# Attention with ALiBi beside a mixture of experts: the order of matmuls in a step, a ring of eight PSUM banks, and values added up in SBUF

## The chip, the core and the metric

The kernel runs on one core of a Trainium2 chip. The metric is device time in microseconds (us); lower is better. Three runs of the kernel before took 1695.01, 1697.31 and 1699.47 us, so the median is 1697.31.

## What is computed

Input `x` has 4 sequences of 1024 tokens with 512 features, all in float32. It is normalized (layer norm without weights), and two branches work on the normalized rows; their outputs are added to the input:

```
xn = layernorm(x)
q, k, v = xn @ Wq.T + bq, ...                    # 16 heads of 32
scores = q @ k.T / sqrt(32); causal mask; scores += -slope[h] * |i - j|
attention = softmax(scores) @ v, heads joined, @ Wo.T + bo
probs = softmax(xn @ gate_w.T); the best 2 of 8 experts, weights scaled to sum 1
expert(t) = (silu(g) * u) @ w2.T,  g, u = split(xn @ w1.T)     # 352 wide
result = x + attention + sum over 2 experts of weight * expert
```

## The kernel before

**Units and groups.** After the norm and the routing, attention runs in 16 units (b, c): a sequence and a chunk of 4 heads (4 x 32 = 128 partitions). A unit has 12 steps, g = 0 to 11. In each step the kernel works on three things of the attention:

- `largest` (L833) for the *next* unit: scores with queries on the partitions, tiles `m`, four matmuls, one per head (L843). A block of 128 queries needs one group of up to 512 keys, or two. DVE adds the distances, takes the least value per query and writes the sum `z` to SBUF (L860). When a block is complete, ACT computes the exponentials of `z` with their sums (`sums`, L880); only the sums are wanted. They go into three bf16 terms each, for shift and inverse (`finish_largest`, `split`, L909), which TensorE turns (`turn_largest`, tile `pt`, L929) into `mT`.
- `scores` (L938): scores with keys on the partitions, tiles `s`, four matmuls (L947), then two kinds of bf16 matmuls that add the shift from `mT` (L958 on the diagonal, L966 with `ones_b`). ACT takes the exponentials (`pr`, L978); on the diagonal POOL clears what is masked (L986).
- `values` (L1015) of the group of the step before: four matmuls that multiply `pr` with the values and add up in one PSUM bank `o` over all groups of a block of 512 queries (L1029). With the last group, `spread_inverse` (L998) spreads the inverses of the sums over the heads' partitions (tile `pi`, four small matmuls, L1003, and a DVE copy `inv`, L1012), and DVE writes `oT = o * inv` (L1039).

The widths differ by step. `s` has 512, 384, 256 and 128 columns in steps 0 to 3, 512 in steps 4 to 8, then 384, 256 and 128. `m` has 128, 256, 384 and 512 in steps 0 to 3, then 512 and 128, 512 and 256, 512 and 384, 512 and 512.

**Shapes on TensorE.** The matmuls of `s` and `m` contract over 32 rows and fill 128 columns (32x128 in the profile); the four heads use the four row strips side by side. `o` contracts over 128 rows and fills 32 columns a head (128x32). All else is 128x128. Every f32 product is two passes in the profile.

**Other work ("fills").** Everything else that TensorE has to do is cut into pieces with estimated lengths: for each of 71 blocks of 128 routed rows `gate` (2.9 us, with the turning of the previous block's activations, `pact`), `up` (2.4) and `second_layer` (3.3: turning of the next rows, `pxs`, and the product `ye` of the block before); the projections of queries, keys and values of later units (`todo`, 3.6 each); and at the end the output projections (3.6) and the joining of expert results on DVE (1.5). A planner, `fill` (L1114), spreads them evenly over gaps, two per step: it keeps a running target (`rate` times the number of gaps) and takes the next piece when the target is reached. The projections of 3.6 are generators that stop halfway (`yield`), so that one half goes into a gap and the other into the next.

**The order of a step** is written out by hand (L1218 to L1230), and each engine follows the program's order: `scores`, `values` of the group before, a gap, the sums on ACT, `largest`, the terms that are due (`run_later`), a gap.

**PSUM.** It has eight banks. Seven are a ring (pool `ps_s`, tag `s`): every tile takes the next one and waits until the tile that had it seven allocations before has been read. The eighth (`ps_o`) holds the routing table first and then `o`.

Of the kernel before, what the change touches and what calls it, by code (L numbers as in the profile page):

```python
# [28 lines left out]
def kernel(  # L29
# [83 lines left out]
    with ExitStack() as actx:  # L113
# [3 lines left out]
        ps_s = actx.enter_context(tc.tile_pool(name="ps_s", bufs=7, space=PSUM))  # L117
        ps_o = actx.enter_context(tc.tile_pool(name="ps_o", bufs=1, space=PSUM))
# [4 lines left out]
        def set_attention():  # L123
# [60 lines left out]
            pick_inv = wp.tile([P, D], BF16, tag="pick_inv", name="pick_inv")  # L184
            for h in range(HC):
                nc.gpsimd.memset(pick_inv[h * D : (h + 1) * D, :], 1.0)
                nc.gpsimd.memset(pick_inv[h * D : h * D + INV, :], 0.0)
# [23 lines left out]
        def project_bias():  # L211


            ps = ps_s.tile([P, E], F32, tag="s", name="pbv")
# [92 lines left out]
        def norm_turn(g):  # L307
# [7 lines left out]
            for n in range(LG):  # L315
                t = g * LG + n
                ptr = ps_s.tile([P, NC, P], F32, tag="s", name=f"ptr{t}")
# [9 lines left out]
        def norm_gate(g):  # L327
            xT = xTs.pop(g)
            plg = ps_s.tile([P, LG * P], F32, tag="s", name=f"plg{g}")
# [15 lines left out]
        def norm_top(g):  # L345
            lgT = lgTs.pop(g)
            plt = ps_s.tile([P, LG, NE], F32, tag="s", name=f"plt{g}")
# [48 lines left out]
        psum = ps_o.tile([P, QB], F32, tag="o", name="routing")  # L396
# [169 lines left out]
        def qk_pieces(b, c):  # L566
# [6 lines left out]
            def piece(which, s):  # L573
                ps = ps_s.tile([P, QB], F32, tag="s", name=f"p{which}_{b}_{c}_{s}")
                for i in range(NC):
# [7 lines left out]
                    if i == NC // 2 - 1:  # L583
                        yield
# [21 lines left out]
        def v_pieces(b):  # L606
            def piece(t):
                ps = ps_s.tile([P, E], F32, tag="s", name=f"pv_{b}_{t}")
                for i in range(NC):
# [7 lines left out]
                    if i == NC // 2 - 1:  # L617
                        yield
# [14 lines left out]
        def expert_pieces():  # L633
# [37 lines left out]
            def turn(k):  # L671
# [4 lines left out]
                ps = ps_s.tile([P, NC, P], F32, tag="s", name=f"pxs_{k}")  # L676
# [5 lines left out]
            def half_up(k, gu):  # L682

                ps = ps_s.tile([P, FI], F32, tag="s", name=f"p{('gate', 'up')[gu]}_{k}")
# [28 lines left out]
            def turn_act(k):  # L713
                if k < 0:
                    return
                ps = ps_s.tile([P, NF, P], F32, tag="s", name=f"pact_{k}")
# [10 lines left out]
            def down(k):  # L727
                if k < 0:
                    return
                y = ps_s.tile([P, E], F32, tag="s", name=f"ye_{k}")  # L730
# [36 lines left out]
        def final_pieces(b):  # L767
# [24 lines left out]
            def project(t, xr, lhsTs):  # L792
                y = ps_s.tile([P, E], F32, tag="s", name=f"y{t}")
                for c in range(NC):
                    nc.tensor.matmul(  # L795
                        y, lhsT=lhsTs[c], rhs=wo_sb[:, c, :], start=(c == 0), stop=(c == NC - 1)
                    )
                    if c == NC // 2 - 1:
                        yield
# [3 lines left out]
            def piece(i):  # L803
# [6 lines left out]
                if o is not None:  # L810
                    return project(t, xr, [o[:, c, :] for c in range(NC)])

            def rest(i):
                cols = slice((i % QT) * P, (i % QT + 1) * P)
                return project(
# [17 lines left out]
        def largest(b, c, g):  # L833
# [6 lines left out]
            for h in range(HC):  # L840
                r = slice(h * D, (h + 1) * D)
                ps = ps_s.tile([P, QB], F32, tag="s", name=f"m_{b}_{c}_{g}_{h}")
# [35 lines left out]
            def sums():  # L878
                for h in range(HC):
                    nc.scalar.activation(  # L880
                        z[h][:, :L],
                        z[h][:, :L],
                        AF.Exp,
                        bias=top[:, h : h + 1],
                        scale=-slopes[c * HC + h],
                        accum_out=total[:, i % QT, h : h + 1],
                    )

            late_sums.append(sums)
# [6 lines left out]
        def run_sums():  # L896
            while late_sums:
# [26 lines left out]
        def turn_largest(b, c, s):  # L924

            t3 = terms[s % 2]
            pt = ps_s.tile([P, QT, P], BF16, tag="s", name=f"pt_{b}_{c}_{s}")
# [10 lines left out]
        def scores(b, c, g):  # L938
# [5 lines left out]
            for h in range(HC):  # L944
                r = slice(h * D, (h + 1) * D)
                ps = ps_s.tile([P, QB], F32, tag="s", name=f"s_{b}_{c}_{g}_{h}")
# [50 lines left out]

        def spread_inverse(b, c, s):  # L998

            ps = ps_s.tile([P, QB], F32, tag="s", name=f"pi_{b}_{c}_{s}")  # L1000
            for h in range(HC):
                r = slice(h * D, h * D + INV + 3)
                nc.tensor.matmul(  # L1003
                    ps[h * D : (h + 1) * D, :],
# [274 lines left out]
```

## Time and profile before

The profiled execution took 1696.5 us; its span (first to last instruction) is 1694.8 us.

| | |
|---|---|
| median of three runs | 1697.31 us |
| profiled execution, its span | 1696.5, 1694.8 us |
| granted clock of TensorE, mean | 0.996 |
| DVE, ACT, POOL busy in unit 5 (92.7 us) | 48.0, 52.5, 14.0 us |
| DVE, ACT, POOL busy in unit 14 (84.5 us) | 59.4, 46.9, 45.9 us |
| idle of TensorE in unit 14 | 4.3 us, nearly all in one wait for the tile `ot` |

In the profile PE is TensorE's matmuls and PEld its weight loads, DVE is VectorE, ACT ScalarE, POOL GpSimd. L947 is line 947 of the kernel. A timeline row gives the start and the length in us, then engine, line, operation, output and inputs, shape (rows*columns of the array, then partitions x columns of the moving operand) and the number of instructions merged. Matmuls overlap in the pipeline, so the length of a row reaches into the next one; the distance from start to start is what a block of matmuls takes. "Busy" counts those lengths, and waits shorter than a drain don't show in it. In the table of groups, the figures behind the bar are the total busy time, the mean length in ns and the idle time of the engine before the group, with what ended it.

### The profile page before, as it was taken

The page shows a single profiled execution, that of the slowest core. Times are in us where ns is not written, and L with a number is a line of the kernel's source. Part 1 is how long each engine was busy: PE and PEld are TensorE (multiplying, and loading weights), DVE is VectorE, ACT ScalarE, POOL GpSimd, SP SyncE. Part 2 cuts the span into 40 slices and gives each one's busy share as a digit, 9 for nine tenths or more (in the row PEclk, how much of TensorE's full clock was granted, in tenths as well). Part 3 has the DMA queues.
Part 4 walks back from the last instruction along what each step waited for, and adds up shares of the span by engine and source line. Part 5 has one row for each costly group of instructions (what it writes and reads, how often), then busy time and mean ns, then how long its engine had stood idle before and what let it go on. Part 6 is the DMA issues. An engine that isn't in the chain of part 4 may idle for free.

```text
span 1694.8 us, 29487 instructions
## 1 busy us (share of the span) xinstructions
PE 1671.3 (99%) x9572; PEld 735.4 (43%) x9572; DVE 914.1 (54%) x2944; ACT 886.7 (52%) x2074; POOL 339.0 (20%) x762
## 2 busy tenths in 40 slices
PE   7999999999999999999999999999999999989999
PEld 4555444444444444444444444444444444433333
DVE  7757555545554545546454545555454545548752
ACT  4353555565464555565455555555555556455531
POOL 5611102021111201021111202011111202035561
PEclk9999999999999999999999999999999999999999
DMA  9747645465343424465443434474434424448881
GB/s 315 312 138 259 213 140 181 157 207 192 129 146 111 126 92 143 154 222 178 135 139 110 130 102 144 140 234 167 147 127 122 135 82 134 135 141 257 245 279 63
DMA packets 146491, 278.99 MB, mean 165 GB/s; under 512 B 16448, under 2 KB 45120, under 8 KB 144800
## 3 DMA queue, kind: packets, MB, share of 16 engines
q1 hardware_dynamic: 132128, 234.60, 42.5%
q0 software_dynamic: 10800, 35.40, 6.9%
q10 hardware_dynamic: 3408, 7.10, 1.1%
q8 instruction: 76, 1.25, 0.3%
q14 instruction: 79, 0.65, 0.2%
HBM read 229.07 MB, written 47.97 MB: 163 GB/s over the span
## 4 chain that ended last, share of the span: by engine, by line
PE 96%; DVE 1%; DMA 1%; issue 1%; POOL 0%; ACT 0%; ACTq 0%; SPq 0%; DVEq 0%
PE ye L733 11%; PE pup L686 11%; PE pgate L686 10%; PE m L843 10%; PE s L947 10%; PE o L1029 9%; PE pk L576 7%; PE pq L576 7%; PE pv L610 7%; PE y L795 6%; PE pxs L679 2%; PE s L966 2%; PE pact L719 2%; PE pt L929 1%; PE pi L1003 1%
## 5 line engine op out<-in xcount | busy, mean ns | idle before, releaser
L978 ACT ACTIVATE pr<-s,kbias 128x512 f32<-128x512 f32 (+3 forms) x768 | 383.1, 582 | 491.1 <-PE s L966 491.0
L880 ACT ACTIVATE z<-z,top 128x896 f32<-128x896 f32 (+7 forms) x512 | 390.0, 777 | 9.2 <-DVE top L873 7.2
L986 POOL TENSOR_SCALAR_AFFINE_SELECT pr<-pr 128x128 f32<-128x128 f32 x512 | 153.8, 309 | 1133.1 <-ACT pr L978 1126.2
L860 DVE CUSTOM_DVE_ANT_0 z<-m,rel 128x512 f32<-128x512 f32 (+3 forms) x512 | 273.0, 587 | 141.9 <-PE m L843 133.2
L733 PE MATMUL ye<-w,actT 128*128 128x512 f32 (+1 forms) x426 | 194.9, 593 | 0.0
L686 PE MATMUL pup<-w,xsT 128*128 128x352 f32 x568 | 185.7, 470 | 0.0
L947 PE MATMUL s<-q,k 32*128 32x512 f32 (+3 forms) x1536 | 181.4, 534 | 0.1
L686 PE MATMUL pgate<-w,xsT 128*128 128x352 f32 x568 | 179.9, 460 | 0.8 <-DVE xsT L680 0.8
L843 PE MATMUL m<-k,q 32*128 32x512 f32 (+3 forms) x1536 | 178.8, 533 | 0.1
L860 DVE CUSTOM_DVE_ANT_0 z<-m,rel,l 128x128 f32<-128x128 f32 (+3 forms) x256 | 125.7, 547 | 81.9 <-PE m L843 80.6
L1029 PE MATMUL o<-pr,v 128*32 128x512 f32 (+3 forms) x1536 | 165.2, 498 | 0.3 <-POOL pr L986 0.3
L686 PEld LDWEIGHTS pup<-w,xsT 128*128 128x128 f32 x568 | 102.8, 190 | 82.5 <-issue 13.7
L576 PE MATMUL pk<-xnT,wk 128*128 128x512 f32 x256 | 127.5, 623 | 0.0
L576 PE MATMUL pq<-xnT,wq 128*128 128x512 f32 x256 | 125.2, 614 | 0.0
L610 PE MATMUL pv<-wv_sb,xnT 128*128 128x512 f32 x256 | 123.6, 612 | 0.0
L686 PEld LDWEIGHTS pgate<-w,xsT 128*128 128x128 f32 x568 | 102.4, 190 | 46.1 <-DVE xsT L680 1.0
L947 PEld LDWEIGHTS s<-q,k 32*128 32x128 f32 x1536 | 62.2, 183 | 128.8 <-issue 60.2
L843 PEld LDWEIGHTS m<-k,q 32*128 32x128 f32 x1536 | 60.4, 182 | 126.3 <-issue 96.2
L733 PEld LDWEIGHTS ye<-w,actT 128*128 128x128 f32 (+1 forms) x426 | 75.5, 191 | 69.5 <-issue 68.3
L880 ACT ACTIVATION_READ_ACCUMULATOR z<-z,top 128x1 f32 x512 | 103.7, 203 | 0.0
L725 ACT COPY actT<-pact 96x128 f32<-96x128 f32 x71 | 18.6, 263 | 151.7 <-DVE actT L722 151.7
L703 DVE SCALAR_TENSOR_TENSOR th<-th,pgate 128x352 f32<-128x352 f32 x71 | 37.0, 522 | 111.2 <-ACT th L702 111.2
(156 smaller groups left out, 1592.9 us busy)
## 6 DMA issues: line engine op xcount, KB each, us to landing
w<-in_w1T SPq DMA_DIRECT2D x284, 352.0 KB, 4.2
w<-in_w2T SPq DMA_DIRECT2D x142, 256.0 KB, 3.0
ys_d<-yr SPq DMA_DIRECT2D x71, 256.0 KB, 2.1
w<-in_w2T SPq DMA_DIRECT2D x71, 192.0 KB, 3.9
xr<-in_x SPq DMA_DIRECT2D x32, 256.0 KB, 4.9
out<-xr SPq DMA_DIRECT2D x32, 256.0 KB, 3.3
xn_d<-xT ACTq DMA_DIRECT2D x6, 1024.0 KB, 8.0
o_d<-oT SPq DMA_DIRECT2D x24, 256.0 KB, 2.6
```

The source lines that it names most:

```text
L576: nc.tensor.matmul(ps, lhsT=ws[which][:, i, :], rhs=xnT[b, s][:, i, :], start=(i == 0), stop=(i == NC - 1),)
L610: nc.tensor.matmul(ps, lhsT=xnT[b, t // QT][:, i, (t % QT) * P : (t % QT + 1) * P], rhs=wv_sb[:, i, :], start=(i == 0), stop=(i == NC - 1),)
L686: nc.tensor.matmul(ps, lhsT=xsT[k][:, c, :], rhs=w1s[k, c][:, gu, :], start=(c == 0), stop=(c == NC - 1),)
L733: nc.tensor.matmul(y, lhsT=a[:m, f, :], rhs=w2s.pop((k, f))[:m, :], start=(f == 0), stop=(f == NF - 1),)
L795: nc.tensor.matmul(y, lhsT=lhsTs[c], rhs=wo_sb[:, c, :], start=(c == 0), stop=(c == NC - 1))
L843: nc.tensor.matmul(ps[:, :n], lhsT=qs[b, c, s][r, (i % QT) * P : (i % QT + 1) * P], rhs=ks[b, c, k0 // QB][r, :n], start=True, stop=True,)
L860: nc.vector.tensor_tensor_reduce(out=zs[h][:, k0 : k0 + n], in0=pss[h][:, :n], in1=rel[:, S - L + k0 : S - L + k0 + n], scale=1.0, scalar= ...
L880: nc.scalar.activation(z[h][:, :L], z[h][:, :L], AF.Exp, bias=top[:, h : h + 1], scale=-slopes[c * HC + h], accum_out=total[:, i % QT, h : ...
L947: nc.tensor.matmul(ps[:, :n], lhsT=ks[b, c, j // QT][r, (j % QT) * P : (j % QT + 1) * P], rhs=qs[b, c, s][r, q0:], start=True, stop=False,)
L978: nc.scalar.activation(pr[:, :n], pss[h][:, :n], AF.Exp, bias=kbias[:, hh, d : d + 1], scale=-slopes[hh],)
L986: nc.gpsimd.affine_select(out=pr[:, :P], in_=pr[:, :P], compare_op=ALU.is_ge, fill=0.0, base=0, pattern=[[1, P]], channel_multiplier=-1,)
L1029: nc.tensor.matmul(o[h * D : (h + 1) * D, q0:], lhsT=vs[b, j][:, col : col + D], rhs=prs[h][:, :n], start=(j == 0), stop=last, skip_group_ ...
```

## The change

- **Order of a step:** `values` of the group before, `scores`, the sums left over, `largest`, the terms that are due, `spread_inverse` where this step's group is the last of its block, `load_wqk`, then one gap for other work, then two of the four sums (the other two follow in the next step after `scores`).
- **Planner:** one gap a step with twice the target (5.0 us of estimated work); the projections are no longer halved. In the 12 steps ahead of unit 0 `largest` comes first, and the gap, the sums after it.
- **PSUM:** during norm and routing the banks are split 7 + 1 as before (`banks`, `hctx`); then both pools are closed and all eight are one ring, from which `o` is taken too (`bank`).
- **Values:** each group's `o` has a bank of its own, started and finished by its four matmuls. DVE copies the first group's into `oT` in SBUF and adds the others to it; with the last group it multiplies `oT` by `inv`.
- **`spread_inverse`:** one 128x128 matmul with a `pick_inv` that has a block for each head, in place of four of 32x32.

The diff, cut to its core (all other hunks replace `ps_s.tile([..], tag="s", ..)` with `bank([..], ..)` and take out the halving):

```diff
+        hctx = ExitStack()
+        banks = {
+            "ring": hctx.enter_context(tc.tile_pool(name="ps_h", bufs=7, space=PSUM)),
+            "routing": hctx.enter_context(tc.tile_pool(name="ps_r", bufs=1, space=PSUM)),
+        }
+
+        def bank(shape, dtype, name):
+            return banks["ring"].tile(shape, dtype, tag="s", name=name)
...
-            pick_inv = wp.tile([P, D], BF16, tag="pick_inv", name="pick_inv")
+            pick_inv = wp.tile([P, P], BF16, tag="pick_inv", name="pick_inv")
+            nc.gpsimd.memset(pick_inv, 0.0)
             for h in range(HC):
-                nc.gpsimd.memset(pick_inv[h * D : (h + 1) * D, :], 1.0)
+                nc.gpsimd.memset(pick_inv[h * D : (h + 1) * D, h * D : (h + 1) * D], 1.0)
...
-            late_sums.append(sums)
+            late_sums.extend(lambda h=h: sums(h) for h in range(HC))
...
-        def run_sums():
-            while late_sums:
+        def run_sums(keep=0):
+            while len(late_sums) > keep:
                 late_sums.pop(0)()
...
-            ps = ps_s.tile([P, QB], F32, tag="s", name=f"pi_{b}_{c}_{s}")
-            for h in range(HC):
-                r = slice(h * D, h * D + INV + 3)
-                nc.tensor.matmul(
-                    ps[h * D : (h + 1) * D, :],
-                    lhsT=pick_inv[r, :],
-                    rhs=mTs[b, c, s][r, :],
-                    start=True,
-                    stop=True,
-                    skip_group_check=True,
-                )
+            ps = bank([P, QB], F32, name=f"pi_{b}_{c}_{s}")
+            nc.tensor.matmul(ps, lhsT=pick_inv, rhs=mTs[b, c, s], start=True, stop=True)
             inv = sp.tile([P, QB], F32, tag="inv", name=f"inv_{b}_{c}_{s}", bufs=1)
             nc.vector.tensor_copy(inv, ps)
-            return inv
+            invs[b, c, s] = inv
...
+            o = bank([P, QB], F32, name=f"o_{b}_{c}_{g}")
             for h in range(HC):
                 col = c * P + h * D
                 nc.tensor.matmul(
-                    o[h * D : (h + 1) * D, q0:],
+                    o[h * D : (h + 1) * D, :n],
                     lhsT=vs[b, j][:, col : col + D],
                     rhs=prs[h][:, :n],
-                    start=(j == 0),
-                    stop=last,
+                    start=True,
+                    stop=True,
                     skip_group_check=True,
                 )
-            if last:
-                oT = sp.tile([P, QB], F32, tag="oT", name=f"oT_{b}_{c}_{s}", bufs=NC * NQ)
-                nc.vector.tensor_tensor(oT, o, inv, ALU.mult)
-                if b == B - 1:
-                    oTs[b, c, s] = oT
-                else:
+            if j == 0:
+                oTs[b, c, s] = sp.tile(
+                    [P, QB], F32, tag="oT", name=f"oT_{b}_{c}_{s}", bufs=NC * NQ
+                )
+                nc.vector.tensor_copy(oTs[b, c, s], o)
+                return
+            oT = oTs[b, c, s]
+            nc.vector.tensor_tensor(oT[:, q0:], oT[:, q0:], o[:, :n], ALU.add)
+            if last_group(g):
+                nc.vector.tensor_tensor(oT, oT, invs.pop((b, c, s)), ALU.mult)
+                if b < B - 1:
                     nc.sync.dma_start(o_d[b * NQ + s][:, c, :], oT)
...
+        def fill(g, todo, count):
+
+            nonlocal spent, gap
             gap += 1
             target = rate * gap
...
+            while todo and (count - len(todo) + 0.5) * NG <= count * (g + 1):
+                todo.pop(0)()
                 spent += PROJ
                 empty = False
             while fills and spent + (0.0 if empty else fills[0][0] / 2) <= target:
...
                 w, f = fills.pop(0)
+                f()
                 spent += w
                 empty = False
...
+        hctx.close()
+        banks["ring"] = actx.enter_context(tc.tile_pool(name="ps", bufs=8, space=PSUM))
...
         for g in range(NG):
-            fill(2 * g, [], 0)
-            run_sums()
             largest(*units[0], g)
             run_later()
-            fill(2 * g + 1, [], 0)
+            fill(g, [], 0)
+            run_sums()
...
             for g in range(NG):
-                scores(b, c, g)
                 if behind is not None:
                     values(*behind)
                 behind = (b, c, g)
-                if g == NG // 2 and n + 3 < len(units):
-                    load_wqk("q", *units[n + 3])
-                fill(2 * g, todo, count)
+                scores(b, c, g)
                 run_sums()
                 if n + 1 < len(units):
                     largest(*units[n + 1], g)
                 run_later()
-                fill(2 * g + 1, todo, count)
+                if last_group(g):
+                    spread_inverse(b, c, S_GROUPS[g][0])
+                if g == NG // 2 and n + 3 < len(units):
+                    load_wqk("q", *units[n + 3])
+                fill(g, todo, count)
+                run_sums(HC // 2)
```

## The prediction

> **What bounds the kernel now.** I first read the busy times and the chain that ended last.
>
> ```profile
> PE 1671.3 (99%) x9572; PEld 735.4 (43%) x9572; DVE 914.1 (54%) x2944; ACT 886.7 (52%) x2074; POOL 339.0 (20%) x762
> ...
> PE 96%; DVE 1%; DMA 1%; issue 1%; POOL 0%; ACT 0%; ACTq 0%; SPq 0%; DVEq 0%
> ```
>
> TensorE is never out of work. DVE and ACT have half of the time free on average. So a change pays only if TensorE streams less or loses less between streams, and it costs wherever TensorE has to wait. What TensorE loses between streams is read from one step in the timeline (start, length, engine, line).
>
> ```profile
> 802.46 2.74 PE L733 MATMUL ye<-w,actT 128*128 128x512 f32 x6
> 805.14 1.14 PE L947 MATMUL s<-q,k 32*128 32x512 f32 x8
> 806.10 0.40 PE L966 MATMUL s<-mT,ones_b 3*128 3x512 bf16 x4
> 806.42 1.06 PE L1029 MATMUL o<-pr,v 128*32 128x512 f32 x8
> 807.42 1.98 PE L576 MATMUL pq<-xnT,wq 128*128 128x512 f32 x4
> 809.34 0.71 PE L843 MATMUL m<-k,q 32*128 32x256 f32 x8
> 809.98 0.40 PE L929 MATMUL pt<-identb,terms 128*128 128x128 bf16 x4
> 810.22 1.94 PE L576 MATMUL pq<-xnT,wq 128*128 128x512 f32 x4
> 812.08 1.14 PE L947 MATMUL s<-q,k 32*128 32x512 f32 x8
> ```
>
> Go by starts: a row's length includes the drain that the next row overlaps. Inside `ye` one pass of 512 columns takes 0.43 us, and an f32 product is two passes; four heads side by side take the time of one. `ye` has six passes, 2.58, and the next row starts 2.68 after it: leaving the shape costs 0.10. `s` has two passes, 0.86, and the ones rows follow after 0.96: entering a shape costs 0.10, which is the first weight load that nothing hides. `s` to ones, both 32x128 in shape, costs nothing. Ones to `o`: 0.32 for a stream of 0.21. `o`: 1.00 for 0.86, since its entry is cheap (0.03) and its exit is not. `pq`: 1.92 for 1.72. `m`: 0.64 for 0.43. From 805.14 to 812.08 it is 6.94 us for 6.01 of streams: **0.93 us a step, in five changes of shape** (full to `s`, to `o`, to full, to `m`, to full). Over the trace the five average 0.95.
>
> **The change, part by part.** There are 16 units of 12 steps, 192 steps; units 0 to 14 also make `m` for the next unit, 180 steps.
>
> *Order of the step.* New order: `o`, `s`, `m`, then all other work. Three changes of shape are left: full to `o` (0.10 + 0.03), `o` to 32x128 (0.11 + 0.11), `m` to full (0.11 + 0.09). That is 0.55 against 0.95, so 0.40 a step, **180 x 0.40 = 72 us less**. The last unit has no `m`, so its two gaps already touch: nothing is gained there, nor in the 12 steps ahead of unit 0 (`m` and other work, two changes before and after).
> The gain rests on `m` following the ones rows at no cost. That pair is not in the trace. The nearest is `s` to ones at 0.00, where the weights came in during the pass before; the other end is a full entry and exit, 0.2. I take 0. The Trainium skill, "TensorE: Matmul & The Clock Gate", part on row and column tiling ("The mechanism"), speaks against this: a weight load overlaps matmuls in flight only when its row group differs, and `m` uses the row groups of the ones rows. By that rule each `m` would pay its load, 0.107 x 180 = 19 us more. The trace's `ye` passes, all in the same rows, follow each other at 0.43 with nothing to see of a load, so I go by the trace.
>
> *pick_inv.* Four 32x32 matmuls with a change of shape of their own (0.32 in 32 places) become one full matmul beside the other work (0.21): **3 us less**. The extra memset on POOL runs once, while TensorE works on routing.
>
> *Values added in SBUF.* A copy or an add from PSUM for each of 192 groups, 0.69 us for 512 columns by these rows, 6.7 us a unit, 107 us of DVE in all. DVE has the room on average (48 of 92.7 us busy in unit 5). What matters is when it gives banks back.
>
> ```profile
> L860 DVE CUSTOM_DVE_ANT_0 z<-m,rel 128x512 f32<-128x512 f32 x320 | 201.9, 687 | 89.2 <-PE m L843 88.5
> L978 ACT ACTIVATE pr<-s,kbias 128x512 f32<-128x512 f32 x384 | 232.6, 689 | 300.9 <-PE s L966 300.9
> L880 ACT ACTIVATE z<-z,top 128x1024 f32<-128x1024 f32 x64 | 72.7, 1151 | 0.0
> L800 DVE TENSOR_TENSOR xr<-y,xr 128x512 f32<-128x512 f32 x32 | 22.1, 690 | 61.3 <-PE y L795 61.0
> ```
>
> *The ring: what is late next.* The order of allocation is now `o`, s0 to s3, m0 to m3, (`pt`, `pi`), first bank of the other work. With eight banks in turn, **the first bank after `m` is s0's**, and m3's is `o`'s. That buffers go round in turn the trace shows: at 1508.4 the four `m` wait for just the tiles seven places back, and m3 starts 0.05 after the exponential that frees its bank.
> Let T be the start of `m`. The first exponential starts at T + 0.26 (0.10 after the ones rows' end) and takes 0.69 for 512 columns, 0.58, 0.48, 0.37 for fewer; s0 is free at T + 1.00, 0.89, 0.78, 0.67. `m` lasts 0.97, 0.75, 0.54, 0.33 for 512 to 128 columns. Where both have 512, all is well. But `m` of 128 meets `s` of 512 in steps 0 and 5, 256 meets 384 in step 1 and 512 in step 7, where `pt` and the piece after it wait in turn. TensorE waits, less the weight load that the wait then hides: 0.56 + 0.24 + 0.56 + 0.75 and 0.03 in four other steps, 2.23 a unit, 15 units: 33 us. The second bank is s1's, a pitch of 0.6 later; where the first piece is only transposes this costs 0.13 to 0.24 more, some 7 us by the planner's order. **40 us.**
>
> *Sums on ACT.* Two of the four sums of a row block now run after the other work, ahead of the next exponentials. With the order worked out from the planner's weights, a gate or key piece ends the work of step 11 in 7 units: its ACT instruction ends 0.65 to 0.85 after TensorE, two sums of 1.15 follow, so the exponentials come 1.2 late (they could start 1.8 after): 7 x 1.2, and smaller ones in steps 2, 3 and 9: **13 us.**
>
> *m3 waits for `o`.* The add is done 0.11 + 0.69 after `o`, and `s` takes 0.97 to 1.24 there: no wait, except where `s` is short. In steps 3 and 11 `s` lasts 0.43; the add of 256 columns, behind the last piece's own DVE work, comes about 0.3 late; 0.05 in steps 2 and 10. 0.7 x 15 = **10 us.**
>
> *One gap.* Pieces that were a gap apart now follow at once. The gate's matmuls wait for `xsT`, which stands in DVE's queue behind four `m` reductions (2.5). Plain steps just make it (4.25 against 4.37 after T). Where the `inv` copy or the term splitting (2.3 us in steps 1 and 5) is ahead too, 0.5 to 1.0 is lost; eight such places: **6 us.**
>
> *Unit 14.* It joins the results while `m` still runs: DVE is busy 59 of 84.5 us before 8 more are added. A step with a projection and a join puts reductions, four multiply-adds of 0.76 and an add on DVE, 7.5 us after T, while TensorE wants m3's bank at 6.1 to 6.8: three times 1.6, and 3 around the first gathers: **8 us.** The 4.2 us wait for `ot` at 1509 stays. The new pool, the first 12 steps and the last multiply: **4.5 us** (bounds 0 and 10).
>
> *SP, POOL.* `load_wqk` moves past `m`, far ahead of its use. The diagonal selects have 0.31 each after the exponentials, and `o` comes a whole gap later than T + 3: nothing.
>
> **Sum.** From the profiled execution's 1696.5 (span 1694.8; the median of the runs is 1697.3, 0.8 above): -72 - 3 + 40 + 13 + 10 + 6 + 8 + 4.5 = +6.5, so 1703; what was left out can only be more waiting, and I say **1704 us**: the switches are saved and nearly all is given back in waits for banks.
>
> **Rivals.**
> *A, faster.* ACT and DVE are half idle, and a wait lets them catch up, so late sums, late adds and late `xsT` overlap one another and cost nothing more. For it: the average load, and that the waits fall in the same steps. Then only the 33 us that follow from the ring alone stay, with 5 for unit 14: 1696.5 - 75 + 38 = 1660. It decides from the point where those sequences cost under 15 us together.
> *B, DVE bound.* DVE is a step behind at every end of the other work, since an add in each step stands ahead of four reductions; then m3 waits 0.3 us in all 180 steps, not in four of twelve: 1704 + 44 = 1748. Against it: 60% load.
> *C, the saving isn't there.* If `m` after the ones rows pays an entry and a drain like any change of shape, half of the 72 goes: 1740. Against it: `s` to ones.
>
> **How the numbers follow.** The main case 0.46, with a range of its own of 1688 to 1720 (bank waits 30 to 50, the others 30 to 50); A 0.28; B 0.15; C 0.11. About 0.3%, 5 us, is what a measurement can tell from no change. Faster by more: all of A and a tenth of the main case, 0.33. Within: 0.11, all of the main case. Slower: the rest of the main case, B and C, 0.56. Eight in ten must take in most of A and of B and C: 1650 to 1745.
>
> **What would show it.** Right: `m` starting 0.21 after the ones rows; TensorE's busy share below 99%, with idle time ahead of the first piece after `m` put down to ACT `pr`, longest in steps 0, 5 and 7; idle ahead of `m` put down to DVE `o`; DVE near 1020 us. Wrong: no idle after `m` (A and more), `m` starting 0.4 after the ones rows (C), or idle ahead of `m` in all steps (B). A bank order other than in turn would undo the main case altogether.

## The result, and the profile after

The changed kernel takes **1719.6 us** (median of four runs, 1718.05 to 1725.33), the kernel before 1697.91 beside it: a ratio of **1.0136, 95% interval 1.0108 to 1.0164**, so 22 to 23 us slower. The forecast was 1704, slower, in a range of 1650 to 1745. The profiled execution took 1718.05 us, its span is 1716.4 (1694.8 before). All sums below are made between these two spans.

The page of the kernel after, the busy times and the engines' shares of the chain that ended last:

```profile
PE 1645.5 (96%) x9476; PEld 779.3 (45%) x9476; DVE 1015.0 (59%) x3136; ACT 892.2 (52%) x2074; POOL 335.0 (20%) x763
...
PE 91%; DVE 3%; ACT 3%; issue 2%; DMA 1%; POOL 0%; ACTq 0%; SPq 0%; DVEq 0%; POOLq 0%
```

TensorE is busy for 26 us less than before, yet the span is 22 us longer: what was saved came back as idle time, and more. ACT has 3% of the chain and DVE 3% (0 and 1% before). DVE is busy for 101 us more, as the values added in SBUF make it.

The same steps as in the forecast's timeline of before, one where all three products have 512 columns and one where `m` has 256 (start, length, work of TensorE, and in brackets the idle time before it with what ended it):

```profile
804.29 1.06 PE L1022 MATMUL o<-pr,v 128*32 128x512 f32 x8
805.29 1.14 PE L948 MATMUL s<-q,k 32*128 32x512 f32 x8
806.25 0.40 PE L967 MATMUL s<-mT,ones_b 3*128 3x512 bf16 x4
806.47 1.04 PE L845 MATMUL m<-k,q 32*128 32x512 f32 x8
807.47 0.55 PE L723 MATMUL pact<-ident,act 128*128 128x128 f32 x3
...
815.15 0.61 PE L845 MATMUL m<-k,q 32*128 32x256 f32 x8
816.15 0.38 PE L930 MATMUL pt<-identb,terms 128*128 128x128 bf16 x4 [0.38 <-ACT pr L979]
816.72 3.70 PE L584 MATMUL pq<-xnT,wq 128*128 128x512 f32 x8 [0.19 <-ACT pr L979]
```

In the first step next to nothing waits. `m` starts 0.22 after the ones rows, whose stream is 0.21: the pair costs nothing, as assumed. From start to start, such a step spends 1.00 (`o`), 1.18 (`s`), 0.97 (`m`) and 0.20 (the other work's exit into `o`), 3.35 together. The row of `m` shows 1.00; I put the 0.03 above 0.97 down to a short wait for the first exponential, which ends at 807.41, where the next row starts at 807.47. Before, `s` with its ones rows, `o`, `m` and two exits of the other work took 1.29 + 1.00 + 1.07 + 0.20 + 0.20 = 3.76. So **0.41 us a step is saved, 0.40 was forecast**. In the second step `m` is done at 815.76 (815.15 + 0.61), but the next bank is that of the first tile of `s`, of 512 columns, and TensorE waits for ACT's exponential: the row of `pt` starts 1.00 after `m` where the streams and the exit take 0.54.

The groups of TensorE in the kernel after that carry the idle time (behind the bar: busy, mean ns, idle before and what ended it):

```profile
L845 PE MATMUL m<-k,q 32*128 32x512 f32 (+3 forms) x1536 | 187.3, 493 | 1.3 <-DVE oT L1037 1.2
L690 PE MATMUL pup<-w,xsT 128*128 128x352 f32 x568 | 182.6, 464 | 7.4 <-ACT pr L979 7.4
L616 PE MATMUL pv<-wv_sb,xnT 128*128 128x512 f32 x256 | 116.9, 601 | 9.1 <-ACT pr L979 9.1
L723 PE MATMUL pact<-ident,act 128*128 128x128 f32 (+1 forms) x213 | 36.4, 279 | 7.6 <-ACT pr L979 7.6
L930 PE MATMUL pt<-identb,terms 128*128 128x128 bf16 x128 | 12.5, 220 | 5.6 <-ACT pr L979 5.6
```

Whatever piece comes first after `m` waits for `pr`, and the idle column shows it. The waits of `m` for the bank of `o` hardly show there (1.3), because most are shorter than the drain of the matmuls before. They show from start to start: added up over the 180 steps, the last head of `m` starts 32.7 us later than the streams need. Where such a late head starts right behind the instruction that frees its bank, that is mostly an add or a copy of `oT` on DVE.

### The profile page after: what moved, and what is told of

Its sections match the earlier page's. It is cut to its first block, busy times and chain, and to the rows that moved or that the text cites. A ratio compares the mean times of both kernels' runs of the same rounds, so it can differ in the third digit from the quotient of the medians.

```text
span 1716.4 us, 29550 instructions
## 1 busy us (share of the span) xinstructions
PE 1645.5 (96%) x9476; PEld 779.3 (45%) x9476; DVE 1015.0 (59%) x3136; ACT 892.2 (52%) x2074; POOL 335.0 (20%) x763
## 4 chain that ended last, share of the span: by engine, by line
PE 91%; DVE 3%; ACT 3%; issue 2%; DMA 1%; POOL 0%; ACTq 0%; SPq 0%; DVEq 0%; POOLq 0%
PE pgate L690 10%; PE pup L690 10%; PE ye L737 10%; PE s L948 9%; PE o L1022 9%; PE m L845 8%; PE pk L584 7%; PE pq L584 7%; PE pv L616 6%; PE y L799 6%; ACT pr L979 2%; PE s L967 2%; PE pxs L683 2%; PE pact L723 2%; PE ptr L327 1%
## 5 line engine op out<-in xcount | busy, mean ns | idle before, releaser
L987 POOL TENSOR_SCALAR_AFFINE_SELECT pr<-pr 128x128 f32<-128x128 f32 x512 | 148.9, 299 | 1123.2 <-ACT pr L979 1116.5
L690 PE MATMUL pgate<-w,xsT 128*128 128x352 f32 x568 | 184.3, 468 | 6.1 <-issue 4.0
L845 PE MATMUL m<-k,q 32*128 32x512 f32 (+3 forms) x1536 | 187.3, 493 | 1.3 <-DVE oT L1037 1.2
L616 PE MATMUL pv<-wv_sb,xnT 128*128 128x512 f32 x256 | 116.9, 601 | 9.1 <-ACT pr L979 9.1
L584 PE MATMUL pk<-xnT,wk 128*128 128x512 f32 x256 | 119.8, 611 | 2.7 <-issue 2.3
L584 PE MATMUL pq<-xnT,wq 128*128 128x512 f32 x256 | 119.2, 609 | 3.1 <-ACT pr L979 3.0
L1037 DVE TENSOR_TENSOR oT<-oT,o 128x512 f32<-128x512 f32 (+3 forms) x160 | 84.0, 525 | 44.0 <-PE o L1022 40.5
L845 PEld LDWEIGHTS m<-k,q 32*128 32x128 f32 x1536 | 93.0, 185 | 32.0 <-DVE oT L1037 12.3
```

What stands on the lines that cost most here:

```text
L584: nc.tensor.matmul(ps, lhsT=ws[which][:, i, :], rhs=xnT[b, s][:, i, :], start=(i == 0), stop=(i == NC - 1),)
L616: nc.tensor.matmul(ps, lhsT=xnT[b, t // QT][:, i, (t % QT) * P : (t % QT + 1) * P], rhs=wv_sb[:, i, :], start=(i == 0), stop=(i == NC - 1),)
L690: nc.tensor.matmul(ps, lhsT=xsT[k][:, c, :], rhs=w1s[k, c][:, gu, :], start=(c == 0), stop=(c == NC - 1),)
L845: nc.tensor.matmul(ps[:, :n], lhsT=qs[b, c, s][r, (i % QT) * P : (i % QT + 1) * P], rhs=ks[b, c, k0 // QB][r, :n], start=True, stop=True,)
L987: nc.gpsimd.affine_select(out=pr[:, :P], in_=pr[:, :P], compare_op=ALU.is_ge, fill=0.0, base=0, pattern=[[1, P]], channel_multiplier=-1,)
```

## The experiments

All ratios are to the kernel before, run beside each; the time of the kernel before differs a little from one set of runs to the next (1696.2 to 1699.9 us), so ratios compare better than times. Diffs are against the changed kernel unless said otherwise. Two sums over the steps of units 0 to 14 are used throughout, both worked out from the starts of the rows. "First piece" is the time that TensorE waits after `m` for the first bank of the other work; it holds the wait for the tile `ot`, 4.1 us in the changed kernel and 4.2 before. "`m` for `o`" is the lateness of the last head of `m` just told. In the changed kernel they are 43.7 and 32.7 us.

**1. `o` in a bank of its own again, a ring of seven, no adds.** It tells the ring from DVE.

```diff
-            o = bank([P, QB], F32, name=f"o_{b}_{c}_{g}")
+            if j == 0:
+                oTs[b, c, s] = banks["o"].tile([P, QB], F32, tag="o", name=f"o_{b}_{c}_{s}")
+            o = oTs[b, c, s]
...
-                    start=True,
-                    stop=True,
+                    start=(j == 0),
+                    stop=last,
...
-        banks["ring"] = actx.enter_context(tc.tile_pool(name="ps", bufs=8, space=PSUM))
+        banks["ring"] = actx.enter_context(tc.tile_pool(name="ps", bufs=7, space=PSUM))
+        banks["o"] = actx.enter_context(tc.tile_pool(name="ps_o", bufs=1, space=PSUM))
```

> The changed kernel with one part undone: o adds up in PSUM in a bank of its own again and the other seven banks are the ring; order and planner stay as changed. Ring theory (the saved shape changes are given back in waits for banks): m3 now comes seven places after s0, so every m waits for the first exponential, T + 1.0 in place of T, some 0.65 us more a step after what the other waits lose: 1780 to 1810 us, with the wait ahead of m put down to ACT pr in all steps. DVE theory (the adds on DVE are what costs): the adds are gone, 107 us of DVE less, so 1640 to 1670 us.

Measured: 1834.7 us, ratio 1.0797 (1.0765 to 1.0829), worse than either theory said, and on the ring's side. The row of `m` and a step of the timeline in this kernel:

```profile
L845 PE MATMUL m<-k,q 32*128 32x512 f32 (+3 forms) x1536 | 308.5, 499 | 42.1 <-ACT pr L979 40.4 <-issue 0.4 <-DMA ys_d<-yr 0.3
```

```profile
703.96 0.39 PE L967 MATMUL s<-mT,ones_b 3*128 3x512 bf16 x4
704.18 0.39 PE L845 MATMUL m<-k,q 32*128 32x128 f32 x6
706.26 0.48 PE L845 MATMUL m<-k,q 32*128 32x128 f32 x2 [1.69 <-ACT pr L979]
```

Four tiles of `s` and four of `m` are eight banks, and the ring has seven: the last head of `m` (its two passes are the "x2") waits for the first exponential of the same step, in every step. In step 0, shown here, ACT has two late sums before that. The adds into SBUF are gone, and it is 115 us worse than the changed kernel. So the eighth bank is what makes this order bearable, and the adds on DVE aren't what bounds it.

**2. The order before, with the rest of the change.** Ring of eight, values added in SBUF, one matmul in `spread_inverse`; order of the step, two gaps and halved projections as before (diff against the kernel before, its core):

```diff
-            o = oTs[b, c, s]
+            o = bank([P, QB], F32, name=f"o_{b}_{c}_{g}")
...
+            nc.vector.tensor_tensor(oT[:, q0:], oT[:, q0:], o[:, :n], ALU.add)
...
+                if last_group(g):
+                    spread_inverse(b, c, S_GROUPS[g][0])
                 fill(2 * g + 1, todo, count)
```

> The kernel before, with the other part alone: the ring of eight, values added in SBUF and the single pick_inv matmul, but the old order of a step and two gaps with halved projections. Ring theory: five shape changes as before and no new waits, since a gap stands between s and m; 1697 less 3 for pick_inv, plus some 5 for the pool that is closed and opened: 1694 to 1705 us, DVE near 1015 us busy. DVE theory: the adds cost the same here as in the changed kernel, 1715 us or more.

Measured: 1693.47 us, ratio **0.9968 (0.9955 to 0.998)**: faster than both kernels. Its page:

```profile
PE 1666.1 (98%) x9476; PEld 736.2 (44%) x9476; DVE 1011.4 (60%) x3136; ACT 886.0 (52%) x2074; POOL 341.6 (20%) x763
```

DVE does all of the added work (1011 us), and TensorE stays busy. In the old order the adds cost nothing; all of the loss lies in the new order, with the single gap and the two late sums that belong to it. (No run has the old order with a single gap, so these aren't parted.)

**3. `m` first: `m`, `s`, `o`, gap.** The first piece then takes a bank of `m`, not of `s`.

```diff
+                held = len(late_sums)
+                if n + 1 < len(units):
+                    largest(*units[n + 1], g)
+                scores(b, c, g)
+                for _ in range(held):
+                    late_sums.pop(0)()
                 if behind is not None:
                     values(*behind)
                 behind = (b, c, g)
-                scores(b, c, g)
-                run_sums()
-                if n + 1 < len(units):
-                    largest(*units[n + 1], g)
```

> The changed kernel with the order m, s, o, gap in place of o, s, m, gap; everything else as changed, so three shape changes a step, the adds on DVE and the single gap stay. Ring theory: o takes m0's bank and the first piece m1's, which DVE has freed while s ran, and m takes banks that were free long ago; the waits of 33 us inside m and 40 us ahead of the first piece go, and late exponentials block nobody: 1635 to 1660 us. DVE theory and gap theory (pieces that follow each other at once are what costs): load and gap are unchanged, 1705 to 1720 us.

Measured: 1731.04 us, 1.0191 (1.0172 to 1.021). A miss. Its row of `o` and a step:

```profile
L1022 PE MATMUL o<-pr,v 128*32 128x512 f32 (+3 forms) x1536 | 163.6, 497 | 20.5 <-DVE l L862 19.2 <-DVE xr L809 0.9
```

```profile
667.01 1.35 PE L948 MATMUL s<-q,k 32*128 32x512 f32 x7
...
668.20 0.59 PE L948 MATMUL s<-q,k 32*128 32x512 f32 x1
```

I had worked out only `o` and the first piece. `o` takes the bank of `m`'s first head and waits for DVE's reduction (19.2 us). And the last head of `s` now stands eight allocations behind the last piece of the gap and waits for that piece's reader, in most steps DVE (`th`, `yr` or `act`): it comes late (the "x1" at 668.20). `s` of 512 columns lasts 1.57 on average, not 1.18. All `s` together lose some 55 us.

**4. Query blocks of `m` in descending order**, so that wide `m` meets wide `s` in step 0.

```diff
-            for i in range(s * QT, (s + 1) * QT)
+            for i in reversed(range(s * QT, (s + 1) * QT))
...
-            if k0 == 0 and i % QT == 0:
+            if k0 == 0 and i % QT == QT - 1:
...
-            if i % QT == QT - 1:
+            if i % QT == 0:
```

> The changed kernel with the query blocks of m taken in descending order, so that wide m meet wide s: widths 512, 384, 256, 128, 512, 512, 512, 384, 512, 256, 512, 128. Ring theory: the waits of the first piece for s0 shrink from 2.2 to 1.3 us a unit and the late sums of 1024 move from the narrow step 0 to step 6: 15 to 25 us less than the changed kernel, 1695 to 1705 us. DVE theory and gap theory: the same work in all, 1715 to 1722 us.

Measured: 1713.76 us, 1.0082 (1.0064 to 1.01): faster than the changed kernel, by less than expected. First piece 43.7 to 18.9 us, about as expected; but `m` for `o` rises to 44.5. It is longest in steps 2 and 6 (0.58 and 0.71 a step). In step 6 of unit 5 the splitting of the terms stands ahead of the add of `o` on DVE: `m` starts at 712.47, the add only at 713.60. In step 2 of that unit it is the last piece's `yr`.

**5. The gap between `s` and `m`:** `o`, `s`, gap, `m`. A change of shape more, but no `m` right behind `s`.

```diff
                 scores(b, c, g)
-                run_sums()
-                if n + 1 < len(units):
-                    largest(*units[n + 1], g)
+                run_sums(HC // 2)
                 run_later()
...
-                run_sums(HC // 2)
+                run_sums()
+                if n + 1 < len(units):
+                    largest(*units[n + 1], g)
```

> The changed kernel with the single gap moved to stand between s and m: o, s, gap, m (the term splitting and the turning go ahead of the gap, two sums after s and two after the gap). Four changes of shape a step in place of three or five: 0.185 us a step less than before, 33 us, and 3 for pick_inv. Ring theory: the first piece and m come long after the banks that they take were read, so the 40 us ahead of the first piece and the waits of m for o go; left is s3 behind the first reduction of m, 1.5 us a unit or 22 us in steps where o is short, and some 12 for the pool and units 14 and 15: 1683 to 1705 us. Gap theory (pieces that follow each other at once cost, wherever the gap stands): 1710 us or more.

Measured: 1719.97 us, 1.0118 (1.0088 to 1.0147). A miss: the 33 us that the shapes should save are all given back. A step of it:

```profile
659.61 1.24 PE L948 MATMUL s<-q,k 32*128 32x512 f32 x7
...
660.69 0.59 PE L948 MATMUL s<-q,k 32*128 32x512 f32 x1
```

Now `m`, `o` and `s` are neighbours round the end of the step, nine banks, and the last head of `s` waits for the reduction of the first head of `m`. It is the wait of experiment 3 in another place; waits of `s` come to 38 us (4.8 of it for `ot`), those inside the gap to 18. By its time the run falls on the side of the gap theory; by its trace the ring has the larger part.

**6. The two sums ahead of the gap.**

```diff
-                fill(g, todo, count)
                 run_sums(HC // 2)
+                fill(g, todo, count)
```

> The changed kernel with the two sums of a step run ahead of the gap in ACT's order, not after it, so that no sum stands ahead of the next exponentials. Ring theory with late sums as I priced them: step 0 falls back from 1.26 us of wait to 0.67 a unit, 9 us less, against a little more wait for the gap's own ACT work (actT, tanh): 1709 to 1716 us. If the late exponentials come from something else than the sums: 1718 to 1722 us, with step 0 as before.

Measured: 1714.77 us, 1.0076 (1.0052 to 1.01), as expected. The start of step 0 of unit 5 in this kernel; the changed kernel has `m` at 661.82 there and the piece at 663.90, 2.08 later, after a wait of 1.68:

```profile
661.73 0.94 PE L845 MATMUL m<-k,q 32*128 32x128 f32 x8
662.77 0.55 PE L723 MATMUL pact<-ident,act 128*128 128x128 f32 x3
```

Half of that wait was two sums that stood on ACT ahead of the exponentials. In step 0 the first piece's wait falls from 18.8 to 8.7 us in all; but in step 1 it rises by 3, and `m` for `o` rises to 38.6, so only some 2 us of waits are gone in the trace. That execution was the longest of its five (1717.94 us); what the others gained beyond it I can't place.

**7. Without the adds.** The line that adds a later group's `o` to `oT` is left out, so the values of all groups but a block's first are lost.

```diff
-            nc.vector.tensor_tensor(oT[:, q0:], oT[:, q0:], o[:, :n], ALU.add)
```

> The changed kernel without the adds of later groups into oT (only the first group of a block is copied and multiplied, the other values are computed and left in PSUM unread): 80 us of DVE less and no reader of o that m3 could wait for. Ring theory: the 29 us that m waits for o go, and a little of the DVE queue in front of xsT and in unit 14: 1684 to 1694 us; the wait of the first piece for s0 stays as it is, 40 us. If DVE's load as a whole were what costs: back to the 75 us that the shapes save, 1635 to 1660 us. If o's bank never mattered: 1715 to 1720 us.

Measured: 1711.42 us, 1.0071 (1.0048 to 1.0094). That is 8 us less than the changed kernel, 11 by the ratios, where 26 to 36 were expected. `m` for `o` falls from 32.7 to 15.0 us, but the first piece's wait rises to 46.0 and those inside the gaps by 5. **A wait taken away brings TensorE earlier to the next bank, which isn't free earlier.**

**8. Experiments 5 and 4 together, with the pools closed late** (experiment 11).

> The gap between s and m as in the run with that order, with the query blocks of m in descending order (narrow m ahead of narrow o, so that s3 finds m0 read) and the first pools closed only after the last projection ahead of the units. Ring theory: s3's wait falls from 22 to some 6 us, and 3 to 5 us of the start are saved: 15 to 22 us less than that order alone, 1665 to 1688 us, faster than both kernels. Gap theory: no better than 1705 us.

Measured: 1716.8 us, 1.0107 (1.007 to 1.0143). A miss, again on the side of the gap theory; the order of experiment 5 isn't saved by this.

**9. Experiment 2 with the pools closed late.**

> The old order with the ring of eight and values added in SBUF, as run before at 1693.5 us, with the first pools closed only after the last projection ahead of the units, so that these matmuls do not wait for the end of the routing. If closing the pools costs what the trace shows (TensorE 3.9 us later at the first projection after it, and a longer stretch at half clock): 1687 to 1691 us. If the time is lost again before the units: 1692 to 1695 us.

Measured: 1690.41 us, 0.997 (0.9959 to 0.9981). The time is in the expected range, but the kernel before was 2 us faster beside it too: the ratio is that of experiment 2, and the late close gains nothing that can be seen there.

**10. The kernel before with `spread_inverse` as one matmul** and nothing else (against the kernel before):

```diff
-            pick_inv = wp.tile([P, D], BF16, tag="pick_inv", name="pick_inv")
+            pick_inv = wp.tile([P, P], BF16, tag="pick_inv", name="pick_inv")
...
-            for h in range(HC):
-                r = slice(h * D, h * D + INV + 3)
...
+            nc.tensor.matmul(ps, lhsT=pick_inv, rhs=mTs[b, c, s], start=True, stop=True)
```

> The kernel before with one part of the change alone: the single 128x128 matmul for the inverses, run ahead of the second gap of the step before it is used; o in PSUM, two gaps, old order. By the price of the shape change in 32 places: 3 us less, 1693 to 1696 us beside 1698 (0.998). If the old order with all other parts gained for another reason (the ring of eight), this one shows no gain.

Measured: 1696.34 us, 1.0000 (0.9991 to 1.0009). The 3 us of the forecast aren't in the time. In the rows they are: from its start to the next one `pi` takes 0.22, where it took 0.325, 3.2 us less over its 32 places. But the ones rows behind `s` take 3.7 us more. A stretch of it:

```profile
589.38 0.38 PE L1002 MATMUL pi<-mT,pick_inv 128*128 128x512 bf16 x1
589.60 1.88 PE L611 MATMUL pv<-wv_sb,xnT 128*128 128x512 f32 x4
591.41 1.21 PE L948 MATMUL s<-q,k 32*128 32x512 f32 x7
592.46 0.37 PE L967 MATMUL s<-mT,ones_b 3*128 3x512 bf16 x1
592.46 0.59 PE L948 MATMUL s<-q,k 32*128 32x512 f32 x1
```

`pi` now takes a bank ahead of the next `s`, so in the ring of seven the last head of `s` stands one place nearer to `m`, and it waits, mostly for DVE's reduction of `m`. In experiment 2, with its ring of eight, `pi` is as short and the ones rows are no longer than before. So this run doesn't show that the single matmul has no part in the gain of experiment 2.

**11. Pools closed after the last projection,** not before the routing's tail:

```diff
-        hctx.close()
-        banks["ring"] = actx.enter_context(tc.tile_pool(name="ps", bufs=8, space=PSUM))
...
         for piece in proj:
             piece()
+        hctx.close()
+        banks["ring"] = actx.enter_context(tc.tile_pool(name="ps", bufs=8, space=PSUM))
```

> The changed kernel with the first pools closed only after the last projection ahead of the units. By the trace 3 to 6 us less than the changed kernel: 1713 to 1717 us. If the start only moves and the units take the time back: 1718 to 1721 us.

Measured: 1711.91 us, 1.0093 (1.0077 to 1.0108), about 7 us less than the changed kernel; the two intervals just touch. In its profile the first unit begins at 185.0 in place of 187.4. That profiled execution was the longest of its four, 1718.62 us at a granted clock of 0.991; the others took 1711.72 to 1711.96 at 0.995. So 2.4 us of the gain are the earlier start; the rest goes with the clock.

**12. Experiments 4, 6 and 11 together,** in the order of the change.

> The changed kernel with three remedies at once that were each run alone: the query blocks of m in descending order, two late sums ahead of the gap, the pools closed after the last projection. Alone they took the ratio to the kernel before from 1.0136 to 1.0082, 1.0076 and 1.0093. If each removes a wait of its own, the three add up: 1.0136 - 0.0054 - 0.0060 - 0.0043 = 0.998, 1694 us. If a wait that is taken away lets TensorE come earlier to the next bank that isn't free, they don't: 1.004 to 1.007, 1705 to 1709 us, with the wait of m for the bank of o (32.7 us in the changed kernel) above 40 us and the wait of the first piece after m (43.7 us) under 20. I expect the second.

Measured: 1699.23 us, 1.0023 (1.001 to 1.0037), between the two expectations: 11.3 thousandths of the 15.7 that the three gained alone. The waits are as I expected (first piece 12.3 us, 5 of it for `ot`; `m` for `o` 45.5), the time is not: most of the gains do add up. In its profiled execution (1696.1 us) units 0 to 13 take 1318.4 us, where the kernel before takes 1325.4 and the changed one 1331.8. So the order of the change can win in the plain units; it loses that again at the start (+4.6), in unit 14 (+1.5) and after it (+0.5). That execution was one of the fastest of twelve, which reach 1706.93; the last section says what they go with.

## Why the forecast was right, and where it wasn't

The terms of its sum, against what the two traces show (us):

| step of the forecast | forecast | measured |
|---|---|---|
| changes of shape, 180 steps | -72 | -74 (0.41 x 180) |
| `pick_inv` | -3 | -3 (its rows, 10.4 before and 7.1 after) |
| first piece after `m`: ring 33, late sums 13 | +46 | +40 (43.7 less 4.1 for `ot`) |
| `m` for `o`: 10, and 5 in unit 14 | +15 | +29 (32.7 less 0.02 a step, by which the last head starts later even without a wait) |
| inside the gap: second bank 7, one gap 6, gathers 3 | +16 | +21 (above 0.19 a step) |
| start and end | +4.5 | +9.5 (start 6.4, after unit 14 3.1) |
| sum | +6.5 | +22.5; the spans differ by 21.6 |

The last line closes to 1 us, and that is in part luck. The middle lines are worked out from the starts of the rows against lengths without a wait, and each is good to some us only: the fifth depends on the 0.19 and has the waits of the kernel before in its own gaps still in it, and the short waits of 0.03 are in no line.

The signs that the forecast named are there: `m` 0.22 after the ones rows, TensorE at 96%, idle time ahead of the first piece put down to `pr` and longest in steps 0, 5 and 7 (step 1 holds the 4.1 us for `ot`), idle time ahead of `m` put down to DVE's `oT`, DVE at 1015 us. So the mechanism is as forecast: the switches are saved, and waits for banks give more than that back. The size is less well met. The waits came out 13 us larger than forecast and the start and end 5, and the range held because it was made wide for the rivals; the main case's own range ended at 1720, which the measured time just meets.

**The saving is there.** The step at 804.29 shows it, and rival C (that `m` pays like any change of shape) falls: in the shorter steps `m` starts 0.11 and 0.05 after the start of the ones rows of 256 and 128 columns (rows below), no more than their streams. The rule of the Trainium skill that the forecast set against it ("TensorE: Matmul & The Clock Gate", "The mechanism": a load overlaps only work in other row groups) would have asked for a load of 0.107 more in each; the rows show none, so here the measurement decides against the rule.

**The ring is what takes it back.** The forecast priced the ring's waits at 0.56 in step 0, 0.24 in step 1, 0.56 in step 5 and 0.75 in step 7 (over two banks there), each per unit. Measured in the changed kernel: 1.26 in step 0, and 0.58 in experiment 6, which has two of the late sums out of the way; 0.24 in step 1 without `ot`; 0.65 in step 5; 0.42 in step 7, and for the second bank in the row of `pq` above another 0.19. Experiment 1 shows that the banks decide it, experiment 4 that widths that match take more than half of it away (43.7 to 18.9 us). Rival A (waits let ACT and DVE catch up, so that 38 us of them stay) falls: 69 us stay behind `m` and ahead of its last head, and 21 inside the gaps. Rival B (DVE bound) falls with experiment 2 and with the steps themselves: in steps 5, 6 and 8 `m` doesn't wait at all.

**The mis-sized step is "m3 waits for `o`: 10 us".** It has twice the size forecast. It named steps 3 and 11 at 0.3 and 2 and 10 at 0.05; measured are 0.45 and 0.42, 0.38 and 0.23, and 0.2 in steps 4 and 9, which it gave nothing. Steps 10 and 11 of unit 4 in the changed kernel, TensorE and then DVE:

```profile
647.29 0.29 PE L967 MATMUL s<-mT,ones_b 3*128 3x256 bf16 x4
647.40 1.24 PE L845 MATMUL m<-k,q 32*128 32x512 f32 x8
648.57 2.63 PE L690 MATMUL pup<-w,xsT 128*128 128x352 f32 x8
...
654.15 0.64 PE L1022 MATMUL o<-pr,v 128*32 128x256 f32 x8
654.72 0.50 PE L948 MATMUL s<-q,k 32*128 32x128 f32 x8
655.05 0.24 PE L959 MATMUL s<-mT,quarter 7*128 7x128 bf16 x4
655.11 0.23 PE L967 MATMUL s<-mT,ones_b 3*128 3x128 bf16 x4
655.16 1.37 PE L845 MATMUL m<-k,q 32*128 32x512 f32 x8
656.47 0.39 PE L1004 MATMUL pi<-mT,pick_inv 128*128 128x512 bf16 x1
```

```profile
654.26 0.69 DVE L746 TENSOR_TENSOR yr<-ye,bo_sb 128x512 f32<-128x512 f32 x1 [1.89 <-PE ye L737]
654.94 0.42 DVE L1037 TENSOR_TENSOR oT<-oT,o 128x256 f32<-128x256 f32 x1
```

`o` is done at about 654.8, but DVE is still at the last piece's `yr` until 654.94, and the add ends at 655.36. The last head of `m`, which starts 0.02 after the first where nothing waits (655.19 here), starts at 655.415: 0.23 late. The block loses more: the last head's second pass starts at 655.949, 0.53 after its first, where these starts are 0.43 apart in the step at 806.47. So `m` takes 1.30 from start to start, not 0.97. Why the second pass falls back by another 0.10 isn't shown. The forecast counted the lateness of the add and left this 0.10 out, and it counted this queue only in steps 3 and 11, though step 10 of the same unit loses 0.20 too (`m` at 647.40, the next row at 648.57: 1.17 for 0.97). In unit 14 the term is 7 us, with joins on DVE, forecast 5.

**The start** was within its bounds (0 to 10). The first projection after the routing in the kernel after:

```profile
105.16 3.75 PE L584 MATMUL pk<-xnT,wk 128*128 128x512 f32 x4 [2.28 <-issue]
```

Before, it starts at 101.31. It waits for the pools to be closed, that is for the last reader of any of their banks. This is DVE's addition of a tile of the first pool, which ends 0.11 earlier:

```profile
104.37 0.68 DVE L1174 TENSOR_TENSOR bo_sb<-bo_sb,pbv 128x512 f32<-128x512 f32 x1
```

Experiment 11 takes that wait away: there the projection starts at 101.73.

**What failed beside it is my view of the remedies.** Experiments 3 and 8 were expected to be faster than before, and 5 by most of its range, because I moved a wait and worked out only the place that it left. With four banks of `s` and four of `m` in turn in a ring of eight, in each of these orders some block stood eight allocations behind one that wasn't read yet. Experiment 12 shows the opposite error: I expected three remedies to undo one another, and most of their gains added up.

**Open:** what makes experiment 2 faster by 0.3%. In its trace the units begin 4.2 us later than before and take 6.7 us less up to the last `s`; 3.2 of these are the rows of `pi`, the rest is spread over many blocks in small amounts. The ring of eight with `o` taken from it can't be had without the adds, so these two aren't parted. Open is also how far the order of the change would go with `o`'s add made early. The best version here is that of experiment 2 or 9: the old order with the new ring.

## What to carry to other kernels

A change of shape on TensorE can be counted from start to start, and putting products of one shape side by side does save it; but each product that moves also moves in the order of the PSUM ring, so for every tile look who has the bank that many allocations earlier, which engine reads it last, and what stands ahead of that on its queue. When a wait is taken away, work out the next one in the same step before pricing the gain: experiment 7 took 18 us of waits from `m` and got 8 to 11 back. And run the parts of a change apart: here the ring, the adds and the single matmul together gained a little in the old order, and the new order lost.

## What the runs showed of the chip that I had not expected

A half-rate clock can stand behind a short wait. In step 0 of unit 9 the changed kernel waits 1.68 us, and the second of these lines, a window (length, busy times, and in the third column from the end the granted clock), comes 2 us later:

```profile
1047.09 0.55 PE L723 MATMUL pact<-ident,act 128*128 128x128 f32 x3 [1.68 <-ACT pr L979]
...
1049.00:1052.00 3.00, 3.00 (x6) 1.73 (x6) 0.00 (x0) 2.24 (x6) 0.13 (x1) 0.51 0.18 69
```

The half-rate stretches in these traces last 3.4 us or two or three times that. There are 13.7 us of them in the kernel before, 23.9 in the changed one, 44 in experiment 1 and 13.7 in experiment 12. The changed kernel's 10.2 us more lie in equal parts ahead of unit 0, in unit 9 and in unit 14. At half rate up to 5 us of its loss may be this; the table doesn't part them from the waits. The same wait in unit 8 had no such stretch behind it, so what decides it stays open.

The executions of one kernel differ in the same way. In experiment 12 those with a granted clock of 0.996 or 0.997 took 1696.1 to 1698.3 us, and those with 0.991 or 0.992 took 1703.2 to 1706.9. The kernel before had 0.995 or more in all but one of its executions beside the experiments (that one, at 0.993, took 1707.5 us), the changed one 0.990 to 0.993. So differences of a few us between experiments 4, 6, 11 and 12 can in part be differences of the clock, and whether an order with more waits is itself the reason for the lower clock isn't shown.
